# A macaron block (FFN, neighbourhood attention, FFN) on one core: weight residuals kept in PSUM and later weight loads at the head, the last softmax first at the tail, and the query residual moved to the front of VectorE's list in every step

## The chip, the core and the metric

The kernel runs on one core of a Trainium2 chip. The core has five engines with instruction queues of their own: PE (TensorE, matrix products), DVE (VectorE), ACT (ScalarE), POOL (GpSimd) and SP (SyncE, which here only issues DMA). Each engine works through its queue strictly in order; semaphores hold an instruction back until what it needs is there. SBUF is the working memory of 128 partitions, PSUM the memory that PE writes its sums to, in banks of 512 f32 values for each partition. The metric is the device time of one execution in microseconds, as the median of several runs.

## The reference, cut to what matters

The input x has 4 batches of 4096 tokens with 512 features. Both FFN halves use the same weight; both are a single linear layer whose two operands are quantised in blocks of 32 to a 6-bit grid.

```python
x = x + 0.5 * ffn(layernorm(x), ffn_weight, ffn_bias)
x = x + attention(layernorm(x), qkv_w, qkv_b, rpb, proj_w, proj_b)
x = x + 0.5 * ffn(layernorm(x), ffn_weight, ffn_bias)

def ffn(x, weight, bias):
    xq, xs = mx_quantize(x)        # scale = max|block of 32| / 7.5, then nearest value of the grid
    wq, ws = mx_quantize(weight)   # a tie goes to the lower value
    return (xq * xs) @ (wq * ws).T + bias

def attention(x, ...):             # 16 heads of 32 features, each query sees 13 neighbours
    q, k, v = split(x @ qkv_w.T + qkv_b);  q = q * SCALE
    a = softmax(q . k[neighbours] + rpb[relative position])
    return (a . v[neighbours]) @ proj_w.T + proj_b
```

## The kernel before

**Arithmetic.** Each f32 operand of a large product is split into two f16 parts, a high part h and a residual l. `product` (L146) adds three products, h·l, l·h and h·h, each over four chunks of 128 features: 12 matmuls of 128x512. A weight or an activation becomes a PE operand in this way: ACT writes h, DVE writes l = value - h, and SP issues a DMA transpose of both.

**Work units.** There are 128 token tiles of 128 tokens (`t`), and 128 attention items (`m`), one for each group of four tiles and each set of four heads. For a tile there are the first norm and quantisation (`quantised_norms`, L220), the first FFN (`first_half`, L277, result `pmf`), the values (`values`, L299, result `pmv`), the output projection (`project_out`, L541, result `pmo`) and the second FFN (`second_half`, L552, also `pmf`). For an item there are the two projections to queries and keys (`project_qk`, L349, results `pmqk`), the scores and softmax (`softmax`, L417, scores `ps`) and the product with the values (`attend`, L488, result `pv`).

**Order.** It is written out by hand. Every stage is a generator; `begin(slot, stage, rank)` (L162) puts it into a slot, and `run_slot` (L165) runs the parts of a slot in order of rank, the lowest first. `yield n, r` means: go on n slots later with rank r. Seven slots (`STEP`) make one step, and each step brings one tile and one item on by one. As every engine runs in order, the rank decides who is in front of whom on DVE, ACT, POOL and SP. What lies ahead of `tc.manual_schedule()` (L772) is ordered by the framework's own scheduler instead.

**Buffers that matter here.** The 128x512 results of PE (`pmf`, `pmv`, `pmo`, `pmqk`) share three PSUM banks (`ps_m`), so each waits until the third result before it has been read. In a step PE makes `pmo`, `pmqk` of the queries, `pv`, `pmqk` of the keys, `pmf` of the first FFN, `pmv`, `pmf` of the second FFN and `ps`; so `pmv` takes the bank of the queries, which the DVE instruction `put_low(0)` (L371 to L375) is the last to read. The residual pair `hlq` of a quantised norm has a single buffer (L259), free when its DMA transpose has landed. The tiles of x come from a pool of 20 (`xp`).

**The query and key part of a step.** In `project_qk` the queries' h part (ACT, L369) is written one slot after its product starts. A slot later, with rank 6, DVE writes the queries' l part and ACT the keys' h part; another slot later DVE writes the keys' l part. In the same slot as the queries' l part stand, with lower ranks, ACT's two normalisations `yq` (L233, rank 1), DVE's `ring` residual of `attend` (L536, rank 0) and the sum, reciprocal and scaling of the softmax (L472 to L474, rank 4).

**The head.** The FFN weight `fw` is quantised in four chunks of 128 rows (L738 to L763): a quotient `wqh` in f16, two subtractions with POOL's products `wu` (L748, L749), a second quotient and a sum (`wq`, L750, L751), the rule for ties (`tie_to_lower`, L136), ACT's rounding to eight bits (L755), POOL's product back into `fw` (L759), and the split and transpose (`whlf`). The other 16 weight chunks (`rows`, loaded into tiles of the x pool in the order `chunks`, L643) are scaled and split by `put_scaled` (L774), one chunk in each slot of the list at L859: slots 2 to 35, in the order v, proj, then q and k in pairs. `attention_bias` (L806) sends the bias of the values through the projection with one more `product`, `pmb`. When slot 38 (`QK`) is reached, the setup pools close, and the buffers of the attention (`p_tile`, cleared at L877, `ring` and others) take their place.

**The tail.** `out_slot` (L573) spreads the output projections of the last tiles; `add_bias` with `after_b` comes five slots before the projection (L602).

Of the kernel before, what the change touches and what calls it, by code (L numbers as in the profile page):

```python
# [64 lines left out]
def macaron_kernel(  # L65
# [66 lines left out]

    def blocks(t):
        return t.rearrange("p (n q) -> p n q", q=QB)

    def tie_to_lower(t):  # L136

        nc.vector.scalar_tensor_tensor(t, t, BELOW_ONE, t, ALU.mult, ALU.min)
        ti = t.bitcast(I32)
        nc.vector.tensor_scalar(ti, ti, 1, None, ALU.bitwise_or)

    def product(pm, lhs, rhs):  # L146

# [201 lines left out]
    def project_qk(m):  # L349

        b, g, c = item_of(m)
        xg = x2[b * NG + g]
        t = qkp.tile([P, 2, 2, KN + GT], F16, tag="qk", name=f"qk{m}")
        qk[m] = t
        pms = []

        def project(s):
            pm = ps_m.tile([P, GT], F32, tag="mm", name=f"pmqk{s}_{m}")
            pms.append(pm)
            o = (QO, KO)[s] + c * P  # L360
            product(
                pm,
                lambda a, kc: wt[:, a, kc, o : o + P],
                lambda a, kc: xg[:, a, kc].rearrange("p i q -> p (i q)"),
            )

        def put_high(s):
            bias = qk_b[:, s, c : c + 1]
            nc.scalar.activation(t[:, s, 0, KN:], pms[s], AF.Identity, bias=bias)  # L369

        def put_low(s):  # L371
            bias = qk_b[:, s, c : c + 1]
            nc.vector.scalar_tensor_tensor(  # L373
                t[:, s, 1, KN:], pms[s], bias, t[:, s, 0, KN:], ALU.add, ALU.subtract
            )  # L375
# [41 lines left out]
    def softmax(m):  # L417

        b, g, c = item_of(m)
        j0, j1 = group_blocks[g]  # L420
        n = j1 - j0
        t = qk.pop(m)
# [43 lines left out]
        yield 1, 4  # L466
        nc.gpsimd.tensor_tensor(s, s, bc(top[:, :n], KN), ALU.subtract)  # L467
        yield 1, 9
        nc.scalar.activation(s, s, AF.Exp, scale=alpha)  # L469
        yield 1, 4  # L470
        total = sm.tile([P, MAXB], F32, tag="total", name=f"total{m}")
        nc.vector.tensor_reduce(total[:, :n], s, AX.X, ALU.add)  # L472
        nc.vector.reciprocal(total[:, :n], total[:, :n])  # L473
        nc.vector.tensor_tensor(total[:, :n], total[:, :n], p_scale[:, :n], ALU.mult)  # L474
        yield 1, 4
# [4 lines left out]
        nc.scalar.copy(ph, s)  # L480
        nc.scalar.copy(p[:, :n, 2 * KN : KV], ph)
        yield 2, 4
# [139 lines left out]
    with tc.tile_pool(name="setup", bufs=1) as sp, tc.tile_pool(name="scratch", bufs=2) as scr:  # L622
# [37 lines left out]
        up = sp.tile([P, 5], F32, name="up")  # L660
        down = sp.tile([P, 5], F32, name="down")

        def powers(lo, hi):

            w = hi - lo
            nc.vector.tensor_reduce(
                top5[:, lo:hi], sq[:, lo * KC : hi * KC].rearrange("p (m c) -> p m c", c=KC),
                AX.X, ALU.max,
            )
            ptn = ps_m.tile([P, 512], F32, tag="mm", name=f"ptn{lo}")  # L670
            nc.tensor.transpose(ptn[:w, :P], top5[:, lo:hi], ident)
            most = sp.tile([w, 1], F32, name=f"most{lo}")
            nc.vector.tensor_reduce(most, ptn[:w, :P], AX.X, ALU.max)
# [6 lines left out]
            e = sp.tile([P, w], I32, name=f"e{lo}")  # L680
            nc.vector.tensor_copy(e.bitcast(F32), pb[:, :w])
            nc.vector.tensor_scalar(e, e, 23, None, ALU.logical_shift_right)
            nc.vector.tensor_scalar(e, e, 131, None, ALU.add)
            nc.vector.tensor_scalar(e, e, 1, None, ALU.logical_shift_right)
            nc.vector.tensor_scalar(e, e, 97, None, ALU.max)
            u, d = up[:, lo:hi].bitcast(I32), down[:, lo:hi].bitcast(I32)
            nc.vector.tensor_scalar(u, e, -1, 264, ALU.mult, ALU.add)
            nc.vector.tensor_scalar(u, u, 23, None, ALU.logical_shift_left)
            nc.vector.tensor_scalar(d, e, -10, None, ALU.add)
            nc.vector.tensor_scalar(d, d, 23, None, ALU.logical_shift_left)  # L690

        powers(4, 5)
        nc.vector.tensor_scalar(cf, down[:, 4:5], 0.5 / XS, None, ALU.mult)
# [39 lines left out]
        def large(name, o, dt=F32):  # L733
            return scr.tile(
                [P, NB, QB], dt, tag=name, bufs=3 if name == "wu_" else KC, name=f"{name}{o}"
            )

        for o in range(KC):  # L738
            fwb = blocks(fw[:, o, :])

            def per(t):
                return bc(t[:, o * NB : (o + 1) * NB], QB)

            qh, q0 = large("wqh_", o, F16), large("wq0_", o)
            nc.vector.tensor_tensor(qh, fwb, per(w_r), ALU.mult)
            for i, b in enumerate((w_hi, w_lo)):
                u = large("wu_", f"{o}_{i}")
                nc.gpsimd.tensor_tensor(u, qh, per(b), ALU.mult)  # L748
                nc.vector.tensor_tensor(fwb, fwb, u, ALU.subtract)  # L749
# [5 lines left out]
            nc.scalar.activation(  # L755
                w8.rearrange("p n q -> p (n q)"), q0f, AF.Copy, scale=1.0 / F8_SCALE,
                saturate=False,
            )
            nc.gpsimd.tensor_tensor(fwb, w8, per(w_back), ALU.mult)  # L759
            hl = scr.tile([P, 2, dim], F16, tag="whl", bufs=4, name=f"whlf{o}")  # L760
            nc.scalar.copy(hl[:, 0, :], fw[:, o, :])
            nc.vector.tensor_tensor(hl[:, 1, :], fw[:, o, :], hl[:, 0, :], ALU.subtract)
            put_weights(4 * KC + o, hl)  # L763

        for t in range(1, EARLY):
# [5 lines left out]

        ctx.enter_context(tc.manual_schedule())  # L772

        def put_scaled(o):  # L774
            s = up[:, o // KC : o // KC + 1]
            hl = scr.tile([P, 2, dim], F16, tag="whl", bufs=4, name=f"whl{o}")
            nc.scalar.activation(hl[:, 0, :], rows[o], AF.Copy, scale=s)
            yield 1, 9
            nc.vector.scalar_tensor_tensor(
# [3 lines left out]

        su, sd = up, down
        tab = sp.tile([P, 1], F32, name="tab")
        vb = sp.tile([P, KC], F32, name="vb")

        def scales():
            powers(0, 4)
# [15 lines left out]

        def attention_bias():  # L806

            vbx = sp.tile([P, 2, KC, P], F16, name="vbx")
            nc.scalar.copy(vbx[:, 0], bc(vb, P))
            nc.vector.tensor_tensor(vbx[:, 1], bc(vb, P), vbx[:, 0], ALU.subtract)  # L810
            yield 3, 9
# [100 lines left out]
```

## Time and profile before

| | us |
|---|---|
| median of three runs | 2440.06 |
| the three runs | 2440.06, 2436.01, 2440.5 |
| the profiled execution, whole | 2436.42 |
| its span, first to last instruction | 2434.6 |
| mean granted PE clock | 0.992 |

The table of stretches (busy time of each engine in a stretch of the span) shows where PE is not full:

| stretch, us | PE | DVE | ACT | POOL |
|---|---|---|---|---|
| 0 to 58 | 2.09 | 49.4 | 26.75 | 33.42 |
| 58 to 110 | 34.93 | 37.95 | 25.31 | 25.83 |
| 100 to 200 | 93.14 | 82.90 | 55.04 | 71.05 |
| 200 to 500 | 292.95 | 258.62 | 169.34 | 253.12 |
| 500 to 800 | 296.62 | 255.29 | 168.10 | 254.56 |
| 1100 to 1400 | 296.42 | 256.45 | 165.79 | 253.86 |
| 2000 to 2300 | 296.00 | 252.75 | 164.12 | 248.75 |
| 2340 to 2435 | 68.95 | 60.89 | 31.67 | 66.93 |

The first two rows and the last are sums of shorter stretches. A page line of instructions reads: line of the kernel, engine, operation, output and inputs, shape and count; after the first bar the busy time in us and the mean in ns; after the second the idle time of the engine just before these instructions, and which instruction ended most of it. In a timeline the first two numbers are start and length in us, and a bracket at the end holds the idle time before the instruction and what ended it.

### The profile page before, as it was taken

What the parts mean: (1) busy time and instruction counts of PE and PEld (TensorE: products, weight loads), DVE (VectorE), ACT (ScalarE), POOL (GpSimd) and SP (SyncE); (2) the same over time, 40 slices, a digit from 0 to 9 for tenths busy, and PEclk for the clock granted to TensorE, in tenths of its full rate; (3) what the DMA queues carried; (4) which work ended last, traced back from release to release, by engine and by line L of the source; (5) the groups of instructions that cost most, each with busy time, mean ns of one, the idle gap of its engine ahead of it and who ended that gap; (6) DMA issues with size and microseconds to landing.
All of it is one profiled execution on the core that took longest, in us unless ns stands there. A gap on an engine that the chain in (4) does not pass through costs nothing.

```text
span 2434.6 us, 82394 instructions
## 1 busy us (share of the span) xinstructions
PE 2295.3 (94%) x35539; PEld 1113.3 (46%) x35539; DVE 2039.3 (84%) x3588; ACT 1321.0 (54%) x2080; POOL 1988.3 (82%) x2012
## 2 busy tenths in 40 slices
PE   0799999999999999999999999999999999999986
PEld 0344444444444444444444444444444444444442
DVE  8788888888888888888888888888888888888776
ACT  4455555555555555555555555555555555555442
POOL 5578888888888888878888888888888888888777
PEclk9899999999999999999999999999999999999998
DMA  5678788787787777778877778777777777777753
GB/s 154 143 145 153 153 161 156 143 152 150 147 159 155 148 147 157 147 144 157 154 146 158 144 152 157 155 148 152 154 140 154 156 157 139 159 148 143 135 110 92
DMA packets 925701, 360.59 MB, mean 148 GB/s; under 512 B 718876, under 2 KB 889752, under 8 KB 925336
## 3 DMA queue, kind: packets, MB, share of 16 engines
q1 hardware_dynamic: 924992, 354.79, 74.4%
q8 instruction: 278, 4.55, 0.8%
q14 instruction: 87, 0.71, 0.1%
q10 hardware_dynamic: 344, 0.53, 0.1%
HBM read 110.15 MB, written 67.29 MB: 73 GB/s over the span
## 4 chain that ended last, share of the span: by engine, by line
PE 67%; DVE 16%; ACT 8%; DMA 5%; issue 3%; POOL 2%; SPq 0%; ACTq 0%; POOLq 0%; DVEq 0%
PE pmf L151 16%; PE pmqk L151 16%; PE pmo L151 13%; PE pmv L151 12%; PE ps L433 6%; DVE total L474 4%; DMA xT<-hlq 4%; DVE total L472 3%; PE pv L503 3%; ACT sf L469 3%; ACT qk L369 2%; DVE qk L373 2%; ACT ring L530 1%; DVE total L473 1%; ACT qk L382 1%
## 5 line engine op out<-in xcount | busy, mean ns | idle before, releaser
L151 PE MATMUL pmf<-wt,xT 128*128 128x512 f16 x3048 | 702.7, 380 | 18.1 <-DMA xT<-hlq 17.7
L151 PE MATMUL pmqk<-x,wt 128*128 128x512 f16 x3072 | 708.6, 380 | 6.0 <-DMA x<-hln 5.3
L151 PEld LDWEIGHTS <-xT 128*128 128x128 f16 x3048 | 296.9, 98 | 386.6 <-DMA xT<-hlq 31.0
L151 PEld LDWEIGHTS <-wt 128*128 128x128 f16 x3072 | 290.2, 98 | 343.3 <-issue 10.2
L246 POOL TENSOR_TENSOR yq<-yq,r 128x1024 f32<-128x1024 f32 (+1 forms) x141 | 246.3, 1747 | 200.5 <-DVE r L244 200.5
L151 PE MATMUL pmv<-wt,x 128*128 128x512 f16 x1536 | 353.5, 380 | 23.5 <-DVE qk L373 14.4
L151 PE MATMUL pmo<-wt,ring 128*128 128x512 f16 x1536 | 356.2, 382 | 2.8 <-issue 2.5
L310 ACT CAST vt<-pmv 128x512 f16<-128x512 f32 x128 | 74.9, 585 | 469.1 <-PE pmv L151 469.1
L564 POOL TENSOR_TENSOR x<-x,half_ffn_b 128x512 f32<-128x512 f32 x256 | 327.3, 1279 | 0.1
L275 DVE SCALAR_TENSOR_TENSOR x<-pmf,coef,x 128x512 f32<-128x512 f32 x256 | 179.7, 702 | 136.9 <-PE pmf L151 136.5
L530 ACT ACTIVATE ring<-pv 128x510 f16<-128x510 f32 (+8 forms) x224 | 82.3, 414 | 368.4 <-PE pv L503 368.4
L180 DVE BATCH_NORM_STATS2 stn<-x 128x6 f32<-128x512 f32 x384 | 265.3, 691 | 9.3 <-DMA x<-in_L_attn_x_dram 0.6
L151 PEld LDWEIGHTS <-x 128*128 128x128 f16 x1536 | 149.9, 98 | 221.6 <-issue 46.4
L251 POOL TENSOR_TENSOR yq<-q,sc 128x1024 f32<-128x1024 fp8e4 (+1 forms) x141 | 246.6, 1749 | 0.0
L249 ACT ACTIVATE q<-yq,nudge 128x1024 fp8e4<-128x1024 f32 (+1 forms) x141 | 150.0, 1064 | 141.6 <-POOL yq L246 133.4
L151 PEld LDWEIGHTS <-ring 128*128 128x128 f16 x1536 | 140.5, 98 | 162.5 <-issue 5.5
L233 ACT ACTIVATE yq<-x,nbq,rsq 128x512 f32<-128x512 f32 x254 | 194.5, 809 | 31.4 <-POOL nbq L192 26.3
L476 POOL TENSOR_TENSOR sf<-sf,total 128x714 f32<-128x714 f32 (+2 forms) x128 | 178.6, 1395 | 37.9 <-DVE total L474 37.4
L483 POOL TENSOR_TENSOR p<-sf,p 128x714 f16<-128x714 f32 (+2 forms) x128 | 192.5, 1504 | 1.2 <-ACT p L480 1.1
L186 POOL TENSOR_SCALAR rsq<-mv 128x2 f32<-128x2 f32 (+1 forms) x141 | 132.0, 936 | 75.0 <-DVE mv L181 72.4
L467 POOL TENSOR_TENSOR sf<-sf,top 128x714 f32<-128x714 f32 (+2 forms) x128 | 180.3, 1409 | 13.8 <-DVE top L465 13.3
L458 DVE TENSOR_TENSOR sf<-ps,table 128x210 f32<-128x210 f32 (+5 forms) x288 | 126.4, 485 | 74.9 <-PE ps L433 74.4
(145 smaller groups left out, 3524.9 us busy)
## 6 DMA issues: line engine op xcount, KB each, us to landing
vs<-vd SPq DMA_DIRECT2D x144, 357.0 KB
x<-in_L_attn_x_dram SPq DMA_DIRECT2D x128, 256.0 KB
vd<-vt SPq DMA_DIRECT2D x128, 256.0 KB
out_dram<-x SPq DMA_DIRECT2D x128, 256.0 KB
vs<-vd SPq DMA_DIRECT2D x24, 378.0 KB
vs<-vd SPq DMA_DIRECT2D x24, 315.0 KB
rows<-in_L_attn_qkv_w_dram SPq DMA_DIRECT2D x12, 256.0 KB
xT<-hlq SPq DMA_TRANSPOSE x141
```

The costliest lines, as they stand in the source:

```text
L151: nc.tensor.matmul(pm, lhs(a, c), rhs(b, c), start=(n == 0), stop=(n == 3 * KC - 1))
L180: nc.vector.bn_stats(st, xs[t])
L233: nc.scalar.activation(y[:, u], xs[t], AF.Identity, bias=nb[:, u : u + 1], scale=rs[:, u : u + 1])
L246: nc.gpsimd.tensor_tensor(yb, yb, bc(r, QB), ALU.mult)
L249: nc.scalar.activation(q8, y, AF.Identity, bias=nudge, saturate=False)
L251: nc.gpsimd.tensor_tensor(yb, q8.rearrange("p u (n q) -> p (u n) q", q=QB), bc(sc, QB), ALU.mult)
L275: nc.vector.scalar_tensor_tensor(xs[t], pm, cf, xs[t], ALU.mult, ALU.add)
L433: nc.tensor.matmul(ps[rows, u, :sides, w * KN : (w + 1) * KN], t[rows, 0, part, q0 : q0 + QR], t[rows, 1, :sides, k0 : k0 + KN], start=par ...
L467: nc.gpsimd.tensor_tensor(s, s, bc(top[:, :n], KN), ALU.subtract)
L476: nc.gpsimd.tensor_tensor(s, s, bc(total[:, :n], KN), ALU.mult)
L483: nc.gpsimd.tensor_tensor(p[:, :n, KN : 2 * KN], s, ph, ALU.subtract)
L564: nc.gpsimd.tensor_tensor(xs[t], xs[t], b, ALU.add)
```

## The change

**Every step.** The queries' l part and the keys' h part go from rank 6 to rank -1, in front of all else in their slot:

```diff
             nc.scalar.copy(t[:, :, :, :KN], halo[:, c])
-        yield 1, 6
+        yield 1, -1
         put_low(0)
         put_high(1)
```

In the queues of a step that gives: on DVE the order hln, queries' l, ring, total (three instructions), keys' l, where it was hln, ring, total, queries' l, keys' l; on ACT the order exp, keys' h, yq, yq, where it was exp, yq, yq, keys' h.

**The tail.** In `softmax` the last item's stages follow each other by one slot with rank -1 (they were two slots apart at two places), and its first stage has rank 0. The `after_b` additions of the last twelve tiles are made early, in the slot where an earlier tile's `after_b` is added, in steps that PE fills:

```diff
+        last_one = m == n_items - 1
+        def step(n):
+            return 1 if last_one else n
+        def rank(r):
+            return -1 if last_one else r
...
-        yield 1, 9
+        yield 1, 9 if m < n_items - 1 else 0
...
-        yield 1, 2
+        yield step(1), rank(2)
...
-        yield 2, 8
+        yield step(2), rank(8)
...
-        begin(at - 5, one(add_bias, t, after_b), 8)
+        begin(min(at - 5, k + 88 if t < LAST - 7 else k + 18), one(add_bias, t, after_b), 8)
```

**The head: the FFN weight.** The value that the four chunks subtract from and divide is a copy `res` in PSUM: three banks of the score tile for chunks 0 to 2, one bank of the `pv` tile for chunk 3; the reciprocals `w_r` are copied to PSUM too. ACT makes the copies, also one more ahead of the last residual, and takes over the multiplication in the rule for ties:

```diff
+        res_s = ps_s.tile([P, 3, 2, 256], F32, tag="s", name="res_s")
+        res_v = ps_v.tile([P, 2, 512], F32, tag="v", name="res_v")
+        r_ps = res_v[:, 1, : KC * NB]
+        nc.scalar.copy(r_ps, w_r)
...
-            nc.vector.tensor_tensor(qh, fwb, per(w_r), ALU.mult)
+            nc.scalar.copy(res, fwf)
+            nc.vector.tensor_tensor(qh, fwb, per(r_ps), ALU.mult)
...
-                nc.vector.tensor_tensor(fwb, fwb, u, ALU.subtract)
-            nc.vector.tensor_tensor(q0, fwb, per(w_r), ALU.mult)
-            nc.vector.tensor_tensor(q0, q0, qh, ALU.add)
+                nc.vector.tensor_tensor(resb, resb, u, ALU.subtract)
+            nc.vector.tensor_tensor(resb, resb, per(w_r), ALU.mult)
+            nc.vector.tensor_tensor(q0, resb, qh, ALU.add)
-            tie_to_lower(q0f)
+            nc.scalar.activation(res, q0f, AF.Copy, scale=BELOW_ONE)
+            nc.vector.tensor_tensor(res, res, q0f, ALU.min)
+            ri = res.bitcast(I32)
+            nc.vector.tensor_scalar(ri, ri, 1, None, ALU.bitwise_or)
...
+            nc.scalar.copy(res, fwf)
-            nc.vector.tensor_tensor(hl[:, 1, :], fw[:, o, :], hl[:, 0, :], ALU.subtract)
+            nc.vector.tensor_tensor(hl[:, 1, :], res, hl[:, 0, :], ALU.subtract)
```

`powers` works on its integers in PSUM in the same way. In the queues that the scheduler makes of this, ACT's copy for chunk 1 stands behind the last copy of chunk 0 and waits for DVE, and so chunk 2 behind chunk 1; chunk 3, in the other tile, starts early.

**The head: the other weights.** The order is now v, then q and k in pairs, then proj, and ten of the 16 chunks come later; `attention_bias` goes from slot 28 to slot 64. The split pairs of the ten later chunks, and the bias operand, lie in tiles of the x pool, and `up`, `down` and `vb` in the lasting pool, since the setup pools close at slot 38:

```diff
-        chunks = (8, 9, 10, 11, 12, 13, 14, 15, 0, 4, 1, 5, 2, 6, 3, 7)
+        chunks = (8, 9, 10, 11, 0, 4, 1, 5, 2, 6, 3, 7, 12, 13, 14, 15)
...
-        for slot, o in zip((2, 4, 5, 6, 10, 13, 16, 19, 21, 23, 25, 27, 29, 31, 33, 35), chunks):
+        for slot, o in zip((2, 3, 5, 6, 20, 24, 29, 31, 36, 38, 45, 48, 52, 55, 57, 59), chunks):
             begin(slot, put_scaled(o), 9)
-        begin(28, attention_bias(), 9)
+        begin(64, attention_bias(), 9)
```

More of the change, by code (lines that the diff above doesn't have):

```diff
@@ L134, in blocks @@
         return t.rearrange("p (n q) -> p n q", q=QB)
[L136 to L144, printed above, removed]
     def product(pm, lhs, rhs):
@@ L465, in softmax @@
         nc.vector.tensor_reduce(top[:, :n], s, AX.X, ALU.max)
-        yield 1, 4
+        yield step(1), rank(4)
         nc.gpsimd.tensor_tensor(s, s, bc(top[:, :n], KN), ALU.subtract)
-        yield 1, 9
+        yield step(1), rank(9)
         nc.scalar.activation(s, s, AF.Exp, scale=alpha)
-        yield 1, 4
+        yield step(1), rank(4)
         total = sm.tile([P, MAXB], F32, tag="total", name=f"total{m}")
@@ L474, in softmax @@
         nc.vector.tensor_tensor(total[:, :n], total[:, :n], p_scale[:, :n], ALU.mult)
-        yield 1, 4
+        yield step(1), rank(4)
         nc.gpsimd.tensor_tensor(s, s, bc(total[:, :n], KN), ALU.mult)
-        yield 2, 8
+        yield step(2), rank(8)
         p = p_tile
@@ L481, in softmax @@
         nc.scalar.copy(p[:, :n, 2 * KN : KV], ph)
-        yield 2, 4
+        yield step(2), rank(4)
         nc.gpsimd.tensor_tensor(p[:, :n, KN : 2 * KN], s, ph, ALU.subtract)
@@ L659, in macaron_kernel @@
         top5 = sp.tile([P, 5], F32, name="top5")
-        up = sp.tile([P, 5], F32, name="up")
-        down = sp.tile([P, 5], F32, name="down")
+        up = const.tile([P, 5], F32, name="up")
+        down = const.tile([P, 5], F32, name="down")
         def powers(lo, hi):
@@ L679, in powers @@
             nc.tensor.matmul(pb[:, :w], ones_w, diag, start=True, stop=True)
-            e = sp.tile([P, w], I32, name=f"e{lo}")
-            nc.vector.tensor_copy(e.bitcast(F32), pb[:, :w])
+            e = pb[:, :w].bitcast(I32)
             nc.vector.tensor_scalar(e, e, 23, None, ALU.logical_shift_right)
@@ L686, in powers @@
             u, d = up[:, lo:hi].bitcast(I32), down[:, lo:hi].bitcast(I32)
[L687 to L690, printed above, removed]
+            f = pb[:, 16 : 16 + w].bitcast(I32)
+            nc.vector.tensor_scalar(f, e, -1, 264, ALU.mult, ALU.add)
+            nc.vector.tensor_scalar(u, f, 23, None, ALU.logical_shift_left)
+            nc.vector.tensor_scalar(e, e, -10, None, ALU.add)
+            nc.vector.tensor_scalar(d, e, 23, None, ALU.logical_shift_left)
         powers(4, 5)
@@ L736, in large @@
             )
+        res_s = ps_s.tile([P, 3, 2, 256], F32, tag="s", name="res_s")
+        res_v = ps_v.tile([P, 2, 512], F32, tag="v", name="res_v")
+        r_ps = res_v[:, 1, : KC * NB]
+        nc.scalar.copy(r_ps, w_r)
         for o in range(KC):
-            fwb = blocks(fw[:, o, :])
+            fwf = fw[:, o, :]
+            fwb = blocks(fwf)
+            res = res_s[:, o].rearrange("p a k -> p (a k)") if o < 3 else res_v[:, 0]
+            resb = blocks(res)
             def per(t):
                 return bc(t[:, o * NB : (o + 1) * NB], QB)
-            qh, q0 = large("wqh_", o, F16), large("wq0_", o)
-            nc.vector.tensor_tensor(qh, fwb, per(w_r), ALU.mult)
+            qh = large("wqh_", o, F16)
+            nc.scalar.copy(res, fwf)
+            nc.vector.tensor_tensor(qh, fwb, per(r_ps), ALU.mult)
             for i, b in enumerate((w_hi, w_lo)):
@@ L748, in macaron_kernel @@
                 nc.gpsimd.tensor_tensor(u, qh, per(b), ALU.mult)
-                nc.vector.tensor_tensor(fwb, fwb, u, ALU.subtract)
-            nc.vector.tensor_tensor(q0, fwb, per(w_r), ALU.mult)
-            nc.vector.tensor_tensor(q0, q0, qh, ALU.add)
+                nc.vector.tensor_tensor(resb, resb, u, ALU.subtract)
+            nc.vector.tensor_tensor(resb, resb, per(w_r), ALU.mult)
+            q0 = large("wq0_", o)
             q0f = q0.rearrange("p n q -> p (n q)")
-            tie_to_lower(q0f)
+            nc.vector.tensor_tensor(q0, resb, qh, ALU.add)
[3 more added lines that the diff above has]
+            nc.vector.tensor_scalar(ri, ri, 1, None, ALU.bitwise_or)
             w8 = large("w8_", o, F8)
             nc.scalar.activation(
-                w8.rearrange("p n q -> p (n q)"), q0f, AF.Copy, scale=1.0 / F8_SCALE,
+                w8.rearrange("p n q -> p (n q)"), res, AF.Copy, scale=1.0 / F8_SCALE,
                 saturate=False,
@@ L760, in macaron_kernel @@
             hl = scr.tile([P, 2, dim], F16, tag="whl", bufs=4, name=f"whlf{o}")
-            nc.scalar.copy(hl[:, 0, :], fw[:, o, :])
-            nc.vector.tensor_tensor(hl[:, 1, :], fw[:, o, :], hl[:, 0, :], ALU.subtract)
+            nc.scalar.copy(hl[:, 0, :], fwf)
+            nc.scalar.copy(res, fwf)
+            nc.vector.tensor_tensor(hl[:, 1, :], res, hl[:, 0, :], ALU.subtract)
             put_weights(4 * KC + o, hl)
@@ L772, in macaron_kernel @@
         ctx.enter_context(tc.manual_schedule())
+        early = chunks[:6]
         def put_scaled(o):
             s = up[:, o // KC : o // KC + 1]
-            hl = scr.tile([P, 2, dim], F16, tag="whl", bufs=4, name=f"whl{o}")
+            if o in early:
+                hl = scr.tile([P, 2, dim], F16, tag="whl", bufs=4, name=f"whl{o}")
+            else:
+                hl = xp.tile([P, dim], F32, tag="x", name=f"whl{o}").bitcast(F16)
+                hl = hl.rearrange("p (s k) -> p s k", s=2)
             nc.scalar.activation(hl[:, 0, :], rows[o], AF.Copy, scale=s)
@@ L785, in macaron_kernel @@
         tab = sp.tile([P, 1], F32, name="tab")
-        vb = sp.tile([P, KC], F32, name="vb")
+        vb = const.tile([P, KC], F32, name="vb")
         def scales():
@@ L806, in attention_bias @@
         def attention_bias():
-            vbx = sp.tile([P, 2, KC, P], F16, name="vbx")
+            vbx = xp.tile([P, dim], F32, tag="x", name="vbx").bitcast(F16)
+            vbx = vbx.rearrange("p (s c q) -> p s c q", s=2, c=KC)
             nc.scalar.copy(vbx[:, 0], bc(vb, P))
```

## The prediction

> **What bounds the kernel now.** I read the busy shares first, then the slices in time, the chain that ended last, the waits of the steady part, and timelines of one step, of the head and of the tail.
>
> ```profile
> PE 2295.3 (94%) x35539; PEld 1113.3 (46%) x35539; DVE 2039.3 (84%) x3588; ACT 1321.0 (54%) x2080; POOL 1988.3 (82%) x2012
> PE   0799999999999999999999999999999999999986
> PE 67%; DVE 16%; ACT 8%; DMA 5%; issue 3%; POOL 2%; SPq 0%; ACTq 0%; POOLq 0%; DVEq 0%
> ```
>
> PE is the bound from the second slice to the last but one. In the stretches 200 to 500, 500 to 800, 1100 to 1400 and 2000 to 2300 of the table it is busy 292.95, 296.62, 296.42 and 296.00 of 300 us, so it loses 4 to 7 us in each, about 33 us over 200 to 2300. Before 58 us it does nothing (2.09 us), and after about 2340 it has gaps. The change adds no matmul: it can only win idle PE time, or add some. What idles PE in the steady part stands in the list of waits, 200 to 2300 us (sum, times, longest):
>
> ```profile
> POOL yq L246 <- DVE r L244: 179.2, 117, 2.0
> DVE x L275 <- PE pmf L151: 120.7, 114, 1.8
> PE pmv L151 <- DVE qk L373: 12.8, 58, 1.1
> ```
>
> One PE wait is large, and it is the one that the moved line touches: `pmv` waits in 58 of about 117 steps, 0.22 us each, for DVE's queries' l part. The timelines of DVE and PE in one step say why:
>
> ```profile
> 1213.16 0.82 DVE L536 SCALAR_TENSOR_TENSOR ring<-pv,ring 128x270 f16<-128x270 f32 x3
> 1214.33 0.94 DVE L472 TENSOR_REDUCE total<-sf 128x18 f32<-128x756 f32 x1 [0.35 <-ACT sf L469]
> ...
> 1215.61 1.28 DVE L474 TENSOR_TENSOR total<-total,p_scale 128x18 f32<-128x18 f32 x1
> 1216.81 1.40 DVE L373 SCALAR_TENSOR_TENSOR qk<-pmqk,qk_b,qk 128x512 f16<-128x512 f32 x2
> ```
>
> ```profile
> 1217.60 2.75 PE L151 MATMUL pmv<-wt,x 128*128 128x512 f16 x12 [0.41 <-DVE qk L373]
> ```
>
> The l part of the queries (the first of the x2) stands behind `ring` and the three `total` instructions, among them a wait of 0.35 us for ACT's exp and an L474 of 1.28 us that takes 0.18 in another step. It ends near 1217.5, and PE starts.
>
> [...] the same subtraction (L749) takes 1.53 or 0.68 us, a shift of 128x4 words (L682, L684) 0.15 or 1.03:
>
> ```profile
> 31.32 1.53 DVE L749 TENSOR_TENSOR fw<-fw,wu 128x512 f32<-128x512 f32 x1
> 34.92 0.68 DVE L749 TENSOR_TENSOR fw<-fw,wu 128x512 f32<-128x512 f32 x1
> 48.44 1.03 DVE L684 TENSOR_SCALAR e<-e 128x4 int32<-128x4 int32 x1
> 54.16 0.68 DVE L762 TENSOR_TENSOR whlf<-fw,whlf 128x512 f16<-128x512 f32 x1
> ```
>
> [...] after 15.22 us idle the 12 matmuls at 58.57 take 4.91 us, and after 4.09 idle those at 159.93 take 5.28, against 2.75 in the product at 63.31. [...]
>
> **The change, part by part.**
>
> *Queries' l first (200 to 2300 us).* In the step shown the l part could start when `hln` ends, about 1213.2: its h part (ACT L369) ran at 1212.55 to 1213.25. It would end near 1214.0 instead of 1217.5, well ahead of PE's 1217.2. The 12.8 us go. Passed over are `ring`, later by 0.7 us (its reader `pmo` is a product of the next step), and `total`, later by 0.35, as 0.35 was a wait for exp. Behind `total` on POOL stands the scaling L476 and then L246, which waits 179.2/117 = 1.5 us a step for `r`: covered. DVE's work ahead of `sc` is the same sum. On ACT the keys' h part (0.67) now stands ahead of both `yq` and waits for the end of the keys' product, 1214.6: `yq` ends about 1216.9 instead of about 1215.9, and `sc`, which needs it, started at 1218.12. If that cover of 1.2 us is gone, the second FFN's `xT` comes late, and PE waits for DMA instead. Bounds: -5 (part comes back as such waits, of which there are 5.2 us already) to -14; I take -12.8.
>
> *Head, to the first product at 58.57.* Removed from DVE's way for the FFN weight: 8 L749 (9.05 us in sum), L745 5.1, L750 4.4, L751 5.3, the tie rule 2.7 and 1.6, L762 2.7: 30.8 us. After it, 32 instructions at the uncontended 0.67 make 21.5, and the small shifts of `powers` (L682 to L688) fall from up to 1 us to 0.15. Nine us of DVE, then, if DVE were the limit. But ACT's new copies wait in order: chunk 1 starts when chunk 0's last copy is done, chunk 2 behind chunk 1. Adding one chunk's own chain (four ACT passes of about 0.65, a fifth of 0.72, eight DVE of 0.67, one POOL of 1.04 and the waits for the queues between) gives some 11 us; walking the queues, I get the last l parts at 32.5, 44.3, 54.0 and 55.1, against 54.84 before. First product: 58.6 ± 2, a gain of 0. If the queues between cost less than I walked, three chunks of 9.5 us instead of 11 would bring it to about 54, so -5 is the best case.
>
> *58 to 106 us.* Ten of 16 chunks, the bias operand, the `after_b` adds and `pmb` are gone or thinner here. DVE loses six instructions of 0.65 to 1.1 before the first `pmqk` (first row below: two in 2.21 us); step by step its work falls by 0.66, 0.76, 1.8 and 2.6, 5.8 in all, and the POOL clearing of `p` loses its wait for DVE (2.22). First `pmqk` at about 101 instead of 106.61: -5.6. Below are timelines of DVE, PE and SP.
>
> ```profile
> 96.10 2.21 DVE L779 SCALAR_TENSOR_TENSOR whl<-rows,up,whl 128x512 f16<-128x512 f32 x2
> ```
>
> ```profile
> 106.61 5.34 PE L151 MATMUL pmqk<-x,wt 128*128 128x512 f16 x24 [1.19 <-DMA x<-hln]
> ...
> 159.93 5.28 PE L151 MATMUL pmqk<-x,wt 128*128 128x512 f16 x12 [4.09 <-DMA x<-hln]
> ```
>
> ```profile
> 154.26 1.25 SPq L205 DMA_TRANSPOSE xT<-hlq  x1
> 155.60 1.29 SPq L205 DMA_TRANSPOSE x<-hln  x1
> ```
>
> *Given back, 106 to 175 us.* What left comes here. Six chunks' DVE passes (0.65 to 0.75) and ACT passes go into steps where DVE is full (12.05 us each by my walk). The weights' transposes now stand on SP among the `xT` and `x<-hln` transposes, 1.3 us of issue each plus their transfer; two stand just ahead of the `x<-hln` whose landing already holds PE 4.09 us (the last row of PE and the SP rows above). I take 3 us for these two. `pmb` (12 matmuls, 2.6 us) moves from idle PE time into full PE time. So of -5.6, -2.4 is left at that `pmqk`, and 0 after `pmb`. Head in sum: 0, from -6 (transposes hidden) to +5 (another cold product).
>
> *Tail.* The last item's subtraction comes 3.7 us earlier, but ACT's copies of `p` (2379.25) stand behind the `hlq` copy that waits for the `xT` landing until 2378.10. Then the `p` residual goes from 2384.5 to about 2380.2, and the last `pv` from 2390.97 to 2386.6. Its `ring` on ACT stands behind another `hlq` copy with such a wait, at 2392.09, itself about 1.8 earlier:
>
> ```profile
> 2378.10 0.62 ACT L200 CAST hlq<-yq 128x512 f16<-128x512 f32 x1 [3.33 <-DMA xT<-hlq]
> 2379.25 0.81 ACT L480 CAST p<-sf 128x756 f16<-128x756 f32 x1
> ...
> 2392.09 0.62 ACT L200 CAST hlq<-yq 128x512 f16<-128x512 f32 x1 [3.81 <-DMA xT<-hlq]
> 2392.62 0.72 ACT L530 ACTIVATE ring<-pv 128x270 f16<-128x270 f32 x3
> ```
>
> So -2 (-1 to -4.3). The early `after_b` adds, 1.28 us of POOL for each of steps 116 to 127, lie in L246's wait of 1.5.
>
> **Sum.** -12.8 + 0 + 0 - 2 = -14.8 us of the profiled execution's 2436.42 (span 2434.6 and 1.8 around it): 2421.6. The median of the runs is 3.6 above that execution, so 2440.06 - 14.8 = 2425.
>
> **Rivals.**
>
> 1. *Another wait takes the place* (0.13). `pmv` no longer waits for DVE, but `yq` comes later by 1 us each step, `xT` with it, and PE stops before the second FFN instead. For it: 5.2 us of that wait are there already, 11 times. Against: 1.2 us of cover. Only the tail stays: 2438.
>
> 2. *The head's gain is kept* (0.20). The late transposes hide behind PE, or the shorter DVE instructions bring the first product forward by up to 5 us. For it: 9 us less DVE in the head. Against: the chunks' serial chain. Head -10: 2415.
>
> 3. *The late weights stop PE* (0.12, slower). Ten chunks' transposes stand in SP's queue between 60 and 175 us; six of them fall where PE is fed step by step through that queue. If the 1.3 us of issue and about 2 of transfer of each reach PE, that is 6 x 3.3 = 20 us[...]: -14.8 + 22.6 = +7.8, 2448. It decides once the head gives up over 15 us, or 4.5 transposes in full.
>
> 4. *The change in PSUM doesn't do what it says* (inside the forecast). The FFN weight gains nothing, because a shared tile puts the three chunks in a row; it costs up to 2 us.
>
> **How the numbers follow.** Forecast 0.55: 2425, its own range 2417 to 2434 (steady -5 to -14, head -6 to +5, tail -1 to -4, not all at one end). The range over all cases is 2412 to 2438. About 0.2% (4.9 us) is what a measurement of this kernel can tell from no change; that puts the bounds at 2435.2 and 2444.9. Faster: nearly all of the forecast (0.53), rival 2 (0.20), 0.03 of rival 1: 0.76. Same: most of rival 1 and what is left of the forecast, and a weak rival 3: 0.13. Slower: 0.11.
>
> **What would show it.** Right: in 200 to 2300 us `pmv` waits for DVE under 2 us in all, the stretches of 300 us show PE at 296 to 298, and PE's waits for `xT` stay near 5. First product within 2 us of 58.6, first `pmqk` near 101, and the `pmqk` that stood at 159.93 2 us earlier at most. Last `pv` near 2386.6 less all that came before. Wrong: PE waits for `xT<-hlq` above 10 us in the steady part (rival 1), a first product before 55 (rival 2), or PE gaps with cold products of 5 us between 106 and 175 that were not there (rival 3).

## The result and the profile after

The changed kernel takes 2469.5 us (median of six runs, 2458.3 to 2478.4) against 2441.9 for the kernel before in the same comparison: a ratio of 1.0105, with a 95% interval from 1.0070 to 1.0139. It is slower by about 28 us, where the forecast was 15 us faster. Its profiled execution took 2467.83 us.

The page of the changed kernel gives these lines. Lines of the code after L145 stand about ten lines higher up than before, so L141 is the former L151, L363 is `put_low` and L359 `put_high`:

```profile
PE 2296.7 (93%) x35539; PEld 1117.2 (45%) x35539; DVE 2011.6 (82%) x3586; ACT 1333.2 (54%) x2093; POOL 1985.6 (81%) x2012
PE   0789999999999999999999999999999999999987
q1 hardware_dynamic: 924992, 354.79, 78.6%
...
PE 82%; DVE 6%; DMA 6%; issue 3%; ACT 2%; POOL 1%; SPq 0%; POOLq 0%; ACTq 0%; DVEq 0%
...
L141 PE MATMUL pmf<-wt,xT 128*128 128x512 f16 x3048 | 706.0, 382 | 36.6 <-DMA xT<-hlq 34.7
L141 PE MATMUL pmv<-wt,x 128*128 128x512 f16 x1536 | 353.9, 380 | 5.0 <-DMA x<-hln 5.0
```

DVE has left the chain (16% before, 6% now), and the wait of `pmv` for DVE is gone: its 23.5 us of idle time are 5.0, all of them in the head. That much came as forecast. But `pmf` now waits 34.7 us for the DMA that brings `xT`; before it was 17.7. The two lines of the kernel before:

```profile
L151 PE MATMUL pmv<-wt,x 128*128 128x512 f16 x1536 | 353.5, 380 | 23.5 <-DVE qk L373 14.4
L151 PE MATMUL pmf<-wt,xT 128*128 128x512 f16 x3048 | 702.7, 380 | 18.1 <-DMA xT<-hlq 17.7
```

The line of the DMA queue holds the clue. Here it is in the kernel before:

```profile
q1 hardware_dynamic: 924992, 354.79, 74.4%
```

The same 924,992 packets with the same bytes took 78.6% of a span that is longer, where they took 74.4%. The packets themselves take longer, and the diff changes neither their number nor their sizes. The waits of PE between 200 and 2300 us (sum, times, longest), in the changed kernel:

```profile
PE pmf L141 <- DMA xT<-hlq: 21.7, 18, 2.8
PE pv L501 <- issue: 13.6, 11, 2.3
PE pmqk L141 <- issue: 9.4, 7, 2.3
PE pmo L141 <- issue: 5.6, 2, 2.8
PE ps L431 <- issue: 2.8, 2, 1.9
```

In the kernel before, the same view has these lines (and two of "issue" with 0.7 and 0.6 us):

```profile
PE ps L433 <- issue: 7.0, 6, 2.5
PE pmf L151 <- DMA xT<-hlq: 5.2, 11, 0.8
PE pmo L151 <- issue: 2.5, 2, 2.0
```

So 5.2 us for `xT` became 21.7, and 10.8 us of "issue" became 31.4. "issue" is time in which PE waits for nothing that the profile shows, and most of it falls inside a product or a group of matmuls: in the timeline of PE two matmuls of a product of twelve run, then nothing for 2.16 us, then the other ten.

```profile
928.34 0.59 PE L141 MATMUL pmqk<-x,wt 128*128 128x512 f16 x2
931.10 3.21 PE L141 MATMUL pmqk<-x,wt 128*128 128x512 f16 x10 [2.16 <-issue]
```

Sorting the DMA packets of the two traces by size shows which are slower (mean time of a packet):

```
bytes   packets   before    after
  256    694272   25.2 ns   26.2 ns
  512    138108   43.1 ns   51.8 ns
 1024     32768   53.6 ns   56.3 ns
 2048     35584   99.5 ns  100.4 ns
```

The packets of 512 bytes are the loads of the values into `vs` (L409 before): one packet for each row of 256 f16 values. The two built programs show what is different about them: the places of the tiles in SBUF. `up`, `down` and `vb` used to lie in the setup pool, which closes. Now they lie in `const`, which is the first pool; each takes a place of 32 bytes there, and every pool behind it moves by 96 bytes. Modulo 256 means the remainder after division by 256; remainder 0 is called "on the grid" below.

```
tile          start before (modulo 256)   start after (modulo 256)
x             65792 (0)                   65888 (96)
hlq, hln, xT  120192, 124288, 126336 (128)  120288, 124384, 126432 (224)
pT            195072 (0)                  195168 (96)
vs            204288 (0)                  204384 (96)
```

So the packets of 512 bytes write to a place that has moved from 0 to 96 modulo 256, and they take 51.8/43.1 = 1.20 times as long. These two traces alone do not show that the one causes the other.

### The profile page after: what moved, and what is told of

Same layout as the page of the kernel before. It is cut to its first block, busy times and chain, and to the rows that moved or that the text cites. A ratio compares the mean times of both kernels' runs of the same rounds, so it can differ in the third digit from the quotient of the medians.

```text
span 2466.0 us, 82317 instructions
## 1 busy us (share of the span) xinstructions
PE 2296.7 (93%) x35539; PEld 1117.2 (45%) x35539; DVE 2011.6 (82%) x3586; ACT 1333.2 (54%) x2093; POOL 1985.6 (81%) x2012
## 3 DMA queue, kind: packets, MB, share of 16 engines
q1 hardware_dynamic: 924992, 354.79, 78.6%
## 4 chain that ended last, share of the span: by engine, by line
PE 82%; DVE 6%; DMA 6%; issue 3%; ACT 2%; POOL 1%; SPq 0%; POOLq 0%; ACTq 0%; DVEq 0%
PE pmqk L141 25%; PE pmf L141 24%; PE pmo L141 14%; PE pmv L141 11%; PE ps L431 6%; DMA xT<-hlq 5%; PE pv L501 3%; DVE qk L363 1%; DVE total L470 1%; ACT ring L528 1%; DVE ring L534 1%; ACT qk L359 1%; DVE stn L170 0%; DVE sc L229 0%; DVE hlq L194 0%
## 5 line engine op out<-in xcount | busy, mean ns | idle before, releaser
L141 PE MATMUL pmqk<-x,wt 128*128 128x512 f16 x3072 | 717.8, 384 | 25.2 <-DMA x<-hln 15.7
L141 PE MATMUL pmf<-wt,xT 128*128 128x512 f16 x3048 | 706.0, 382 | 36.6 <-DMA xT<-hlq 34.7
L141 PEld LDWEIGHTS <-xT 128*128 128x128 f16 x3048 | 297.2, 98 | 408.7 <-DMA xT<-hlq 51.7
L141 PEld LDWEIGHTS <-wt 128*128 128x128 f16 x3072 | 291.6, 99 | 370.1 <-issue 43.3
L141 PE MATMUL pmo<-wt,ring 128*128 128x512 f16 x1536 | 358.9, 384 | 9.3 <-issue 5.6
L141 PE MATMUL pmv<-wt,x 128*128 128x512 f16 x1536 | 353.9, 380 | 5.0 <-DMA x<-hln 5.0
L363 DVE SCALAR_TENSOR_TENSOR qk<-pmqk,qk_b,qk 128x512 f16<-128x512 f32 x256 | 190.8, 745 | 72.9 <-ACT qk L359 71.9
L241 POOL TENSOR_TENSOR yq<-q,sc 128x1024 f32<-128x1024 fp8e4 (+1 forms) x141 | 246.9, 1751 | 2.5 <-ACT q L239 2.5
L141 PEld LDWEIGHTS <-x 128*128 128x128 f16 x1536 | 150.5, 98 | 187.6 <-DMA x<-hln 5.5
L141 PEld LDWEIGHTS <-ring 128*128 128x128 f16 x1536 | 141.3, 99 | 170.9 <-issue 13.3
L359 ACT ACTIVATE qk<-pmqk,qk_b 128x512 f16<-128x512 f32 x256 | 176.1, 688 | 65.1 <-PE pmqk L141 65.1
L223 ACT ACTIVATE yq<-x,nbq,rsq 128x512 f32<-128x512 f32 x254 | 192.9, 803 | 22.2 <-POOL nbq L182 21.7
```

Of the source, the lines that this page charges most:

```text
L141: nc.tensor.matmul(pm, lhs(a, c), rhs(b, c), start=(n == 0), stop=(n == 3 * KC - 1))
L223: nc.scalar.activation(y[:, u], xs[t], AF.Identity, bias=nb[:, u : u + 1], scale=rs[:, u : u + 1])
L241: nc.gpsimd.tensor_tensor(yb, q8.rearrange("p u (n q) -> p (u n) q", q=QB), bc(sc, QB), ALU.mult)
L363: nc.vector.scalar_tensor_tensor(t[:, s, 1, KN:], pms[s], bias, t[:, s, 0, KN:], ALU.add, ALU.subtract)
```

## The experiments

Three theories stood: the addresses; the order (`yq`, and so `xT`, late because of the keys' h part, the first rival of the prediction); and the head's late weights (the third). A mark in the traces helps to split the time: the start of the queries' product of item m. Between items 20 and 112 lie 92 steps without head or tail.

### Addresses, order, or head

*The changed kernel with its tiles back at their places modulo 512:*

```diff
+        const.tile([P, 104], F32, name="pad")
         up = const.tile([P, 5], F32, name="up")
```

> The changed kernel with one more unused tile of 416 bytes in the lasting pool, so that every later tile lies at the same place modulo 512 as in the kernel before (moved by 512 bytes in all, not by 96). Address theory (the lasting tiles up, down and vb moved vs, pT, x and xT by 96 bytes, and the DMA packets that write them take longer): the 512-byte packets fall back from 51.8 to about 43 ns, the DMA share of the steady part from 0.83 to 0.78, PE's waits of 200 to 2300 us from about 55 to 20-33 us, and the time to 2425 to 2447 us (20 to 45 less than the 2469 of the changed kernel). Order theory (queries' l first makes yq and so xT late, and DMAs bunch): as the changed kernel, 2465 to 2475. Head theory (the late weight transposes cost it all): as the changed kernel too.

*The kernel before with 96 bytes more:*

```diff
+        const.tile([P, 24], F32, name="pad")
         up = sp.tile([P, 5], F32, name="up")
```

> The kernel before with one unused tile of 96 bytes in the lasting pool and nothing else, so that every later tile lies where the changed kernel has it. Address theory: slower than before by 15 to 35 us (2455 to 2475), 512-byte packets about 52 ns, DMA share 0.83 between 200 and 2300 us. Order theory and head theory: no change, 2435 to 2445.

*The kernel before with the new rank alone:*

```diff
-        yield 1, 6
+        yield 1, -1
```

> The kernel before with the rank of the queries' l part and the keys' h part at -1 alone; no tile moves. Address theory together with the forecast's first step: faster by 5 to 14 us (2427 to 2436), pmv's waits for DVE gone, xT waits still about 5 us. Order theory: slower by 10 to 25 us (2450 to 2465), with PE waiting for xT 15 us or more. Head theory: faster by 5 to 14.

*The changed kernel with the rank back at 6:*

```diff
-        yield 1, -1
+        yield 1, 6
```

> The changed kernel with the rank back at 6; the new head and tail and the moved tiles stay. Address theory: the time stays high, 2465 to 2490, as the slow packets stay. Order theory: back to 2436 to 2446. Head theory: 2470 to 2485.

The kernel before took 2441.3 us beside these four.

```
                             median us   ratio (95%)              512 B      one step
after, places back           2422.8      0.9916 (0.9900, 0.9932)  43.9 ns    17.84 us
before, 96 bytes more        2489.1      1.0194 (1.0177, 1.0211)  50.7 ns    18.44 us
before, new rank             2408.6      0.9872 (0.9855, 0.9890)  43.6 ns    17.82 us
after, rank 6                2495.3      1.0219 (1.0204, 1.0233)  50.7 ns    18.46 us
(before                      2441.3                               43.1 ns    18.03 us)
(after                       2469.5                               51.8 ns    18.21 us)
```

The address theory holds. The cost of the addresses and the gain of the rank are both larger than I expected: all four times lie beyond the ranges given for this theory, the first by 2 us, the others by 5 to 18. An unused tile of 96 bytes alone makes the kernel before 48 us slower, and taking that shift out of the changed kernel gives 47 us back. The order theory falls: the new rank alone is 33 us faster. The head theory falls too: the second run has the old head, and is slow all the same. The waits of PE from 200 to 2300 us in the kernel before with 96 bytes more look like those of the changed kernel:

```profile
PE pmf L151 <- DMA xT<-hlq: 22.2, 20, 2.4
PE ps L433 <- issue: 11.1, 7, 4.1
PE pmv L151 <- DVE qk L373: 11.0, 49, 1.1
PE pmqk L151 <- issue: 7.1, 6, 1.7
PE pv L503 <- issue: 6.2, 7, 1.9
PE pmo L151 <- issue: 3.6, 2, 3.4
```

`xT` and "issue" are high without any part of the change. The sign that the prediction named for its first rival (waits for `xT` above 10 us) came true for another reason.

### Which tile, and which grid

*The kernel before with 64 bytes more, and then (64 values in place of 16) with 256:*

```diff
+        const.tile([P, 16], F32, name="pad")
         up = sp.tile([P, 5], F32, name="up")
```

> The kernel before with an unused tile of 64 bytes in the lasting pool, so that vs and pT start at 64 modulo 256 and all other tiles move by 64 too. If the packets' cost goes by blocks of 256 bytes [...]: as slow as with 96 bytes, 2475 to 2495, 512-byte packets 50 ns or more. If it goes by 64-byte lines: no change, 2435 to 2447, packets 43 to 44 ns.

> The kernel before with an unused tile of 256 bytes: every tile moves, but keeps its place modulo 256. By blocks of 256 bytes: no change, 2435 to 2447, packets of 512 bytes at 43 to 44 ns. If it were the moving itself, or a grid of 512 bytes: slower by 15 us or more.

*The kernel before with 96 bytes in a pool just ahead of `vs`:*

```diff
+    pvs = ctx.enter_context(tc.tile_pool(name="pvs", bufs=1))
+    pvs.tile([P, 24], F32, name="pvs_pad")
     vsp = ctx.enter_context(tc.tile_pool(name="vsp", bufs=2))
```

> The kernel before with 96 unused bytes just ahead of the tile vs alone, so that only vs leaves the 256-byte grid. If the 512-byte packets into vs are the cost: as slow as with all tiles moved, 2475 to 2492, packets of 512 bytes at 50 ns or more. If it is pT, x or the other tiles: 2436 to 2455, and if both, in between.

*The new rank, and two pools `phl` and `ppt` of 128 and 384 bytes that put the other tiles that DMAs read or write in every step on the grid (`wt`, written in the head alone, stays at 160):*

```diff
-        yield 1, 6
+        yield 1, -1
...
+    phl.tile([P, 32], F32, name="phl_pad")
     hlp = ctx.enter_context(tc.tile_pool(name="hlp", bufs=1))
...
+    ppt.tile([P, 96], F32, name="ppt_pad")
     ptp = ctx.enter_context(tc.tile_pool(name="ptp", bufs=2))
```

> The kernel before with the rank at -1, and 128 unused bytes ahead of hlq and 384 ahead of pT, so that hlq, hln, xT, vt and ring, which stood at 128 modulo 256, stand on the 256-byte grid too (vs and pT stay on it). If reads and writes of these tiles pay for being off the grid as vs does: faster than the order alone (2408.6) by 5 to 20 us, packets of 256 and 1024 bytes shorter than 25.7 and 53.8 ns. If only the 512-byte packets into vs pay: 2403 to 2414.

The kernel before took 2441.0 us here.

```
                             median us   ratio (95%)              512 B     256 B     one step
all tiles by 64              2483.9      1.0181 (1.0153, 1.0209)  49.4 ns   25.7 ns   18.38 us
all tiles by 256             2436.8      0.9988 (0.9979, 0.9997)  43.1 ns   25.3 ns   18.04 us
vs alone by 96               2484.1      1.0188 (1.0154, 1.0221)  50.7 ns   25.4 ns   18.37 us
new rank, all on the grid    2401.1      0.9842 (0.9821, 0.9863)  43.3 ns   22.3 ns   17.74 us
```

It is the place, not the moving, and not a line of 64 bytes: with 256 bytes more the packets of 512 bytes stay at 43.1 ns and the ratio is 0.9988, with 64 bytes more they take 49.4 ns and the ratio is 1.0181, nearly that of 96 bytes (1.0194). (No run has `vs` at 128.) Moving `vs` alone costs 43 of the 48 us, and the two intervals overlap: nearly all of the cost, if not all, is that one tile's. PE does not read the moved tile more slowly: in the 92 steps its matmuls of `ps` and `pv`, without stops over 0.7 us, take 151.4 us before and 151.7 with `vs` moved. Against 43.1 ns on the grid the 512-byte packets take 49.4/43.1 = 1.15 times as long from 64, and 50.7/43.1 = 1.18 from 96.

The last run carries it further. In the kernel before, `hlq`, `hln`, `xT`, the tile `x2` that takes the transposes of `hln`, `vt`, `ring` and `p` stood at 128 modulo 256. On the grid, the 256-byte packets (the transposes') fall from 25.7 ns (new rank alone) to 22.3, a ratio of 25.7/22.3 = 1.15. The share of the DMA queue falls from 76.1% with the new rank alone to

```profile
q1 hardware_dynamic: 924992, 354.79, 70.1%
```

and the waits of PE (200 to 2300 us) are

```profile
PE ps L435 <- issue: 5.9, 3, 2.2
PE pv L505 <- issue: 3.8, 4, 1.5
PE pmqk L153 <- issue: 2.3, 3, 1.3
PE pmf L153 <- DMA xT<-hlq: 1.5, 3, 1.1
```

The wait for `xT` is 1.5 us, where the new rank without this had 9.5:

```profile
PE pmf L151 <- DMA xT<-hlq: 9.5, 11, 1.3
```

The median is 7.4 us below that run's, but the two intervals touch, so the time alone doesn't prove this smaller gain; the packets and the step (17.82 to 17.74 us) agree with it. At 2401.1 us this version is faster than both kernels.

### Head and tail on the grid

Each part was put alone on that last version: the FFN weight with `powers` in PSUM; the ten late weights and the late bias, with `up`, `down` and `vb` in `const` and 416 bytes beside them; and the tail's edits. Their diffs are those shown of the change.

> All tiles on the 256-byte grid and the rank at -1, as in the run before it of that kind (2401.1 us; queries of item 0 start at 105.3 us of the span, of item 6 at 183.0), with the FFN weight's residuals in PSUM alone; the other weights keep their slots. If the three chunks in a row cost what the forecast left out: first product 1 to 3 us later than 58.6, item 6 at 183 to 186. If the late weights alone cost the head: first product and item 6 unchanged within 1 us. Time 2398 to 2405 either way.

> The same, with the ten later weights and the later bias alone (up, down and vb in the lasting pool with 416 bytes more, so that the tiles stay on the grid). If the weight transposes in SP's queue cost the head: item 0 at about 101 (4 us earlier), but item 6 at 186 to 189 (3 to 6 us later), the wait for hln of item 4 near 9 us, time 2403 to 2409. If they are hidden: item 6 at 183 or earlier, time 2395 to 2401.

> The same, with the tail's edits alone. Forecast's step: 1 to 4 us shorter from item 127 (82.9 us from there to the end), time 2397 to 2400. If ACT's and POOL's queues take it back: 0 to 2 us longer, 2401 to 2404.

And the whole change, with 416 bytes in `const`, and 128 and 384 ahead of `hlq` and `pT`:

> The whole changed kernel with 416, 128 and 384 unused bytes, so that x, hlq, hln, xT, vt, ring, pT and vs all stand on the 256-byte grid. If the head and the tail bring nothing and cost nothing once the addresses are right: 2398 to 2408, as with the order alone on the grid (2401.1). If they cost what they seemed to cost off the grid for xT (2422.8 against 2408.6): 2409 to 2418.

```
                  median us  ratio (95%)              item 0    item 5    item 8    item 127 to end
rank, on the grid 2401.1     0.9842 (0.9821, 0.9863)  105.3     170.6     214.2     82.9
+ FFN weight      2402.3     0.9837 (0.9810, 0.9865)  105.4     171.1     213.3     83.1
+ late weights    2403.8     0.9854 (0.9822, 0.9886)   98.3     172.4     214.3     82.9
+ tail            2407.1     0.9858 (0.9829, 0.9887)  106.3     171.7     214.0     83.2
the whole change  2406.2     0.9852 (0.9833, 0.9871)  101.1     174.3     216.2     83.2
```

All five intervals overlap. The tail's median lies above both ranges that were expected of it, and the late weights start item 0 earlier than expected. The marks say where each part goes. The late weights bring item 0 forward by 7.0 us and have lost all of it, and 1.8 more, at item 5. PE's timeline in that run shows how, at items 0 and 4:

```profile
98.34 7.20 PE L153 MATMUL pmqk<-x,wt 128*128 128x512 f16 x24 [6.20 <-DMA x<-hln]
...
154.95 5.28 PE L153 MATMUL pmqk<-x,wt 128*128 128x512 f16 x12 [7.25 <-DMA x<-hln]
```

The wait for `hln` at item 4 is 7.25 us; without the late weights it is 3.74. In the changed kernel itself, where the packets are slow as well, it is 9.32. There DVE has written `hln` at 146.57 us, and SP issues its transpose at 157.80; in between two of the weights' transposes hold SP's queue for 5.9 us:

```profile
145.89 0.68 DVE L194 TENSOR_TENSOR hln<-yn,hln 128x512 f16<-128x512 f32 x1
```

```profile
146.51 5.88 SPq L695 DMA_TRANSPOSE wt<-whl  x2
152.44 0.58 SPq L166 DMA_DIRECT2D x<-in_L_attn_x_dram  x1
153.12 3.24 SPq L483 DMA_TRANSPOSE pT<-p  x1
156.46 1.25 SPq L195 DMA_TRANSPOSE xT<-hlq  x1
157.80 1.30 SPq L195 DMA_TRANSPOSE x<-hln  x1
```

With the late weights alone on the grid `hln` lies ready for 9.7 us before its transpose is issued (142.41 to 152.07), without them for 6.6 (145.63 to 152.25). At item 4 the product still starts 1.5 us earlier with them (154.95 against 156.49). Up to item 5 come `pmb`, 12 matmuls or 2.6 us of PE, and 0.8 us that the product of item 4 takes longer (5.28 us behind the wait of 7.25, 4.44 behind that of 3.74).

In the tail run the last `pv` comes 36.1 us after the queries of item 127 instead of 38.8, 2.7 us earlier. Then PE waits, as PE's and ACT's timelines of that run show:

```profile
2362.41 14.55 PE L153 MATMUL pmo<-wt,ring 128*128 128x512 f16 x57 [3.18 <-ACT ring L540]
```

```profile
2361.44 0.62 ACT L202 CAST hlq<-yq 128x512 f16<-128x512 f32 x1 [4.28 <-DMA xT<-hlq]
2361.96 0.72 ACT L540 ACTIVATE ring<-pv 128x270 f16<-128x270 f32 x3
```

The last `ring` stands on ACT behind an `hlq` copy that waits 4.28 us for a transpose to land, and the earlier `pv` is given back there: that `ring` starts 40.3 us after the queries of item 127, against 40.2 without the tail's edits.

## Why the prediction was wrong, by its own steps

**The step that failed is the sum, -12.8 + 0 + 0 - 2: it has no term for where the tiles lie.** The prediction counted instructions and DMAs that the change adds, removes and moves. That three small tiles go to the first pool was told in the description of the change, and costed at nothing. They moved every later tile by 96 bytes and `vs` with them off the grid, which costs 48 us with the old rank (the run with 96 bytes more; `vs` alone 43) and 47 with the new (2469.5 - 2422.8). It outweighs all that was forecast. The slow cases in the prediction named other causes, and none of them holds the 28 us. The 22.6 us in its third rival are the 20 us of the transposes and 2.6 us for one product behind a long wait; that 2.6 was the author's estimate, and the two such products in the trace of before took 2.16 and 2.53 us more than the 2.75 at 63.31.

**Queries' l first: the right mechanism, with a size too small.** Forecast -12.8, bounded at -14; measured alone, -32.7 (2441.3 to 2408.6). The wait did vanish, in the changed kernel too. Its size was read from the idle column, which counts idle time from the modelled end of the matmul before. A matmul here lasts 380 ns in the groups, but in a product the next one starts 216 ns after it. So the first 163 ns of each wait stay hidden. Start to start, the trace of before has on average 481 ns ahead of the first `pmv` matmul; 265 ns are lost in each of the 92 steps, 24.4 us, where the idle column has 12.7 for the same steps. At 265 ns the 128 steps lose 34 us. Some 51 ns of each step come back ahead of the second FFN (277 to 328 ns start to start), so the rival's later `xT` is real but small. The traces thus show 214 ns a step, 27 us in 128 steps; the medians differ by 33 us, the two profiled executions by 21. The prediction's 33 us of idle PE between 200 and 2300 us leave out the hidden part in the same way.

**Head: forecast 0; at item 8 it is 2 us late on the grid, and 6 off it.** First product forecast at 58.6 ± 2, measured 60.98 in the changed kernel, outside that, and 58.3 with the FFN weight alone on the grid (57.6 without it): the edits save DVE 9.4 us up to 58 us (49.41 to 40.03 busy), as forecast, and PE nothing. That the 32 instructions would take 0.67 us each with an operand in PSUM was the author's estimate. In the trace of before, the instructions of L749 to L751 have both inputs in SBUF: the five from 25.51 to 32.85 us take 1.52 or 1.53 us each, while POOL works without a stop up to 32.31, and those at 43.16 and 45.63 take 0.67, while POOL is idle. (Two at 36.54 and 37.14 take 0.67 and 0.68 beside POOL's L759, which takes 2.38 us there and 1.04 to 1.49 the other three times.) In the changed kernel L757, L758, L761 and L765, with one input in PSUM, take 0.68 to 0.70 us each, L758 at 22.42 us, for one, 0.69 beside POOL's L241 (22.14 to 23.19). The OR of the tie rule takes 0.69 us in PSUM; in SBUF it took 0.41. Item 0 was forecast at about 101: 102.4, and 101.1 with the places back. The giving back was forecast with the right transposes and too small, 3 us for two that hold SP for 5.9: at item 4 a product at 161.22 us, not 157.5. (By its own terms, 5.6 - 3, the prediction had 2.6 us left there, not the 2.4 it wrote.) On the grid item 8 stands 2.0 us later with the whole change (214.2 to 216.2); off the grid it is 6 us later than before (223.3 against 217.3). How much of that comes from the slower packets, and how much from the transposes, was not shown.

**Tail: forecast -2, measured +0.3** between item 127 and the end, on the grid (2.5 us longer in the changed kernel itself: 86.0 against 83.5). The order of events was right up to the last `pv`. The step that failed is that the `hlq` copy ahead of the last `ring` would come 1.8 us earlier: it comes 39.8 us after the queries of item 127, against 39.7 without the tail's edits.

**The account.** Order -33, head and tail +14 (2422.8 - 2408.6; the two intervals leave it between about 5 and 17, and the spans of the profiled executions show 6.6), addresses +47: together +28. The three add up because they are one chain of runs, each compared with the one before it; they are not independent. With the tiles moved the new rank gains 26 us (2495.3 to 2469.5), and on the grid head and tail cost 5 (2401.1 to 2406.2), which the intervals don't tell from nothing.

## What to carry to other kernels

After any edit to a pool that others follow, compare where the large DMA targets start, modulo 256 bytes: an unused tile of 96 bytes cost this kernel 2%, and two pads in the right places, with the new order, gave the lowest median measured here (2401.1 us). When the same packets and bytes take a larger share of the DMA engines (here 78.6% after 74.4%), look at addresses before looking for a new wait. And read PE's waits from start to start: here, with matmuls of 380 ns that start 216 ns apart, the idle time left out the first 163 ns of each wait.

## What the runs showed of the hardware

**PE stops inside products: 6 times before, 18 and 17 times in the two kernels with slow packets.** Between items 8 and 116 I took every pair of matmuls of the same product or group that start more than 0.7 us apart. The kernel before has 6 of them (8.5 us), the changed one 18 (31.7 us), before with 96 bytes more 17 (28.3 us). In the changed kernel each of the 18 ends 1.3 to 1.9 us after a packet of one of the instruction queues (8 or 16 KB) has ended; of moments drawn at random only 8% lie so. That is a coincidence in time; what stops PE there was not shown.

**The cost does not stand at `vs`.** In steps 20 to 112 the 96 bytes cost the kernel before 37.4 us, counted from start to start: 19.0 stand ahead of `pmf`, mostly as waits for `xT`, and 14.4 are the stops over 0.7 us inside products and groups. Another 6.7 us are 33 matmuls that start about 419 ns apart instead of 216; the wait of `pmv` is 2.7 us shorter. No wait for `vs` itself stands in the list of PE's waits. How the slower loads of `vs` (50.7 ns a packet) come to hold up `xT` was not shown.

**With stops of about 2 us PE's granted clock was at times one half.** 29 of the 33 slow matmuls lie in three stretches of 3.4 to 6.8 us in which the granted clock is one half. The changed kernel has seven such stretches of 3.4 us between 200 and 2300 us, and the kernel before none. Each of the seven begins 2.0 to 4.1 us after the start of a stop of PE of 1.90 to 2.83 us, as here after the 2.16 us shown above (PE's clock is the number before the last two):

```profile
core 0: us, PE busy (x) PEld busy (x) DVE busy (x) ACT busy (x) POOL busy (x), PEclk, DMA share, GB/s
925.00:928.30 3.30, 3.30 (x112) 1.89 (x98) 2.73 (x6) 3.10 (x5) 3.30 (x3) 1.00 0.94 172
932.40:935.80 3.40, 3.40 (x76) 1.42 (x75) 0.42 (x1) 0.76 (x2) 3.23 (x5) 0.50 1.11 161
```

Other stops as long (2.77 us at 1784.6 in the changed kernel, 2.49 at 1041.2 in the kernel before) are followed by none. What decides between the two was not shown.
